# Two columns per product: summing the messages of a graph kernel in two PSUM halves

## Chip, cores and metric

The kernel runs on one core of one Trainium2 chip. The metric is the device time of one launch in microseconds (us), as the median of several runs of the same program; less is better.

## What is computed

The input is a graph of N = 6250 nodes with F = 256 numbers each, and E = 100000 edges, sorted by their destination. Three attention layers follow one another. Cut to what matters:

```python
def gatv2(x, src, dst, Wl, Wr, att, b):     # 4 heads of 64; src, dst with self loops added
    xl, xr = (x @ Wl).reshape(n, 4, 64), (x @ Wr).reshape(n, 4, 64)
    e = leaky_relu(xl[src] + xr[dst], 0.2)
    logits = einsum('ehc,hc->eh', e, att)
    alpha = softmax of logits over the edges of each dst
    return segment_sum(xl[src] * alpha[:, :, None], dst).reshape(n, 256) + b

def gat(h, W, a, src, dst):                 # 8 heads of 32, no self loops
    Wh = h @ W;  s1, s2 = Wh . a[:, :32], Wh . a[:, 32:]
    e = leaky_relu(s1[src] + s2[dst], 0.2)
    attn = softmax of e over the edges of each dst
    return segment_sum(attn[:, :, None] * Wh[src], dst).reshape(n, 256)

h = gatv2(elu(gatv2(x, first weights)), second weights)
x = layernorm(x + h)
return layernorm(x + gat(x, W, a))
```

All numbers are fp32. The part that the change touches is the weighted `segment_sum` at the end of each layer.

## The kernel before

`tile_gnn_kernel` (L634) first makes a plan on the chip (`make_plan`, L699): nodes are sorted by the number of their edges and laid into NB = 49 blocks of 128, one node on each partition. Block b has `cols[b]` edge columns, as many as its busiest node has edges: 38 in the first, then 25, 24, down to 9 in the last, 814 in all. The plan also makes the first layer's table of xl in DRAM. As the graph fits this plan, `tile_by_degree` (L1121) does the rest; another path, for graphs that don't fit, is in the program but not run. Both parts stand under a manual schedule: each engine executes its instructions in the order in which the program text issues them, and an instruction that has to wait holds up all that stand behind it on its engine.

**Layers 1 and 2** are one function, `layer2` (L1261), called for i = 0 and 1; layer 3 is written out from L1445 on in the same form. Each goes once over the 49 blocks. For a block:

- `gather` (L1277, L1451): GpSimd (POOL) issues one indirect DMA per column; each fetches, for all 128 partitions, the table row of that column's source node (256 numbers and some more) into SBUF. The columns of a block are cut into 2 to 5 chunks of at most T = 9 (`chunks`, L1189), each in a row tile g; there are 7 such tiles in layers 1 and 2, and 8 in layer 3. The gathers of block b + 1 are issued ahead of the work on block b. In layers 1 and 2 the node's own row is an additional column, which is not gathered: 814 + 49 = 863 columns a layer.
- `attend` (L1295, L1462): VectorE (DVE) makes the logits lg. In layers 1 and 2 that takes three passes over each chunk (maximum L1302, multiplication L1303, sum L1304). `weights` (L1194) takes the maximum over the columns ("top", L1198), and ScalarE (ACT) the exponentials wt into PSUM: in layers 1 and 2 four instructions, one per head, which sum the denominator den too (L1205); in layer 3 one instruction (L1215), and DVE sums den (L1218).
- `end(b - 1, ...)` (L1317, L1476) finishes the block before: DVE multiplies that block's sum acc, read from PSUM, with its reciprocal den and writes h (L1319, L1478); then follow bias or residual, and in layers 2 and 3 the layer norm's statistics (L1247, L1249), with the root by ACT (L1251).
- DVE takes the reciprocal of den (L1348, L1514).
- `weighted_sum` (L1223): the gathered rows are multiplied in place with their weights. In layers 1 and 2 ACT scales the last 3 to 8 columns, one instruction of 64 numbers for each head and column (L1234), with a copy "by" of the weights; DVE scales the others, a chunk at a time (L1235). Behind the first chunk, `between` runs what is left of block b - 1 on DVE and ACT. Then TensorE (PE) adds the columns: one product of each column with the identity, all accumulating into the same 256 numbers per partition of the PSUM tile acc (L1242). In fp32 a product is two passes, each with a weight load of its own, so that the 863 + 863 + 814 = 2540 products appear as 5080 matmul records. acc has one buffer in layers 1 and 2, and three in layer 3.
- In layers 1 and 2 the last step of block b - 1 comes behind the products of block b: transposes on TensorE, a copy of their result by ACT (xT, L1182), products with the next weights (L1187), a copy of the row by ACT, and its store to DRAM, issued by SyncE (SP). In layer 3 the finished rows y (by ACT, L1259) are written to the output by an indirect DMA from POOL (`put_out`, L1493; L1496), which stands in POOL's order behind the gathers of block b + 1 and writes the rows of block b - 2.

So in each block's order the sum of block b - 1 is taken up by DVE after the logits of block b and ahead of its scalings.

Of the kernel before, what the change touches and what calls it, by code (L numbers as in the profile page):

```python
# [23 lines left out]
F32 = mybir.dt.float32  # L24
# [8 lines left out]
P = 128  # L33
# [1087 lines left out]
def tile_by_degree(  # L1121
# [3 lines left out]
    nc = tc.nc  # L1125
    N, F = x.shape
    H2, D2 = att1.shape
    H1, _, D1 = w3.shape
    NB = -(-N // P)
# [12 lines left out]
    def per_head(t, H):  # L1142
        return t.rearrange("p (h d) -> p h d", h=H)
# [78 lines left out]

    def weighted_sum(ps, rows, cut, wts, H, width, between):  # L1223

        wt, by = wts
        acc = ps.tile([P, F], F32, name="acc")
        S = cut[-1][1]
        for g, (s0, s1) in zip(rows, cut):
            n = s1 - s0
            g4 = g[:, :n, : H * width].rearrange("p t (h d) -> p t h d", h=H)[:, :, :, : F // H]  # L1230
            m = n - by.shape[1] if by is not None and s1 == S else n
            for t in range(m, n):
                for h in range(H):
                    nc.scalar.mul(g4[:, t, h, :], g4[:, t, h, :], by[:, t - m, h : h + 1])  # L1234
            nc.vector.tensor_mul(  # L1235
                g4[:, :m], g4[:, :m],
                wt[:, s0 : s0 + m, :].unsqueeze(3).to_broadcast([P, m, H, F // H]),
            )
            if s0 == 0:
                between()  # L1240
            for t in range(n):
                nc.tensor.matmul(acc, ident, g4[:, t], start=s0 + t == 0, stop=s0 + t == S - 1)  # L1242
        return acc

    def spread_of(work, t):
        stats = work.tile([P, nc.vector.BN_STATS_DIM], F32, name="stats")
# [14 lines left out]
    def layer2(i, table, of, width, start, own, finish):  # L1261

        with ExitStack() as es:
            rowp = es.enter_context(tc.tile_pool(name=f"rows{i}", bufs=7))
            zp = es.enter_context(tc.tile_pool(name=f"z{i}", bufs=3))
            work = es.enter_context(tc.tile_pool(name=f"work{i}", bufs=3))
            ps = es.enter_context(tc.tile_pool(name=f"ps{i}", bufs=2, space=PSUM))  # L1270
            ps1 = es.enter_context(tc.tile_pool(name=f"ps1{i}", bufs=1, space=PSUM))
            pst = es.enter_context(tc.tile_pool(name=f"pst{i}", bufs=2, space=PSUM))
            at = ps1.tile([P, W2], F32, name="at")
            nc.scalar.copy(at, att[i])
            state = {}

            def gather(b):  # L1277
                cut = chunks(cols[b] + 1)
                rows = [rowp.tile([P, T, width], F32, name="g") for _ in cut]
                for g, (s0, s1) in zip(rows, cut):  # L1280
                    for s in range(max(s0, 1), s1):
                        nc.gpsimd.indirect_dma_start(  # L1282
                            out=g[:, s - s0, :], out_offset=None, in_=table,
                            in_offset=source(of, b, s - 1),
                        )
                state[b] = [rows, cut]

            later = []

            def ready(b):  # L1290
                pr, put = own(work, ps, pst, b, state[b][0][0][:, 0, :W2])
                state[b].append(pr)
                later.append(put)

            def attend(b):  # L1295
                rows, cut, xr = state.pop(b)
                S = cols[b] + 1
                lg = work.tile([P, CM + 1, H2], F32, name="lg")
                for g, (s0, s1) in zip(rows, cut):
                    n = s1 - s0  # L1300
                    z = zp.tile([P, T, W2], F32, name="z")[:, :n, :]
                    nc.vector.tensor_max(z, g[:, :n, :W2], xr[:, None, :].to_broadcast([P, n, W2]))  # L1302
                    nc.vector.tensor_mul(z, z, at[:, None, :].to_broadcast([P, n, W2]))  # L1303
                    nc.vector.reduce_sum(  # L1304
                        lg[:, s0:s1, :], z.rearrange("p t (h d) -> p t h d", h=H2), axis=AX.X
                    )
                few = min(S // 3, cut[-1][1] - cut[-1][0] - 1) if b + 1 < NB else 0
                wt, new = weights(work, ps, lg, S, H2, few)
                while later:
                    later.pop()()  # L1310
                if i == 0:
                    for g, (s0, s1) in zip(rows, cut):
                        s = max(s0, 1)
                        nc.scalar.copy(spots[:, b, s - 1 : s1 - 1], g[:, s - s0 : s1 - s0, W2])
                return rows, cut, wt, new

            def end(b, acc, den):  # L1317
                h = work.tile([P, F], F32, name="h")
                nc.vector.tensor_mul(  # L1319
                    per_head(h, H2), per_head(acc, H2),  # L1320
                    den.unsqueeze(2).to_broadcast([P, H2, D2]),
                )
                if i == 0:
                    nc.vector.tensor_add(h, h, bias[0])
                return finish(work, pst, b, h)

            for b in range(3):
                start(work, b)
            gather(0)
            ready(0)  # L1330
            later.pop()()
            if i == 0:
                none(state[0][2])
            acc, den, rest = None, None, None
            for b in range(NB):
                if b + 3 < NB:
                    start(work, b + 3)
                if b + 1 < NB:
                    gather(b + 1)
                if b + 1 < NB:  # L1340
                    ready(b + 1)
                rows, cut, wt, new = attend(b)
                if b:
                    rest = end(b - 1, acc, den)
                if i == 0:
                    nc.vector.tensor_add(x1[:, b, :], x1[:, b, :], bias[1])
                den = new()
                nc.vector.reciprocal(den, den)  # L1348

                last = []  # L1350

                def between():
                    if b:
                        last.append(rest())

                acc = weighted_sum(ps1, rows, cut, wt, H2, D2 + 1, between)
                if i == 0 and b + 1 < NB:
                    none(state[b + 1][2])
                if last:
                    last[0]()  # L1360
            end(NB - 1, acc, den)()()

    def none(t):

# [80 lines left out]
    with ExitStack() as es:  # L1445
        rowp = es.enter_context(tc.tile_pool(name="rows3", bufs=8))
        work = es.enter_context(tc.tile_pool(name="work3", bufs=3))
# [11 lines left out]
                    )  # L1459
            state[b] = (rows, cut)  # L1460

        def attend(b):  # L1462
            rows, cut = state.pop(b)
            S = cols[b]
            lg = work.tile([P, CM, H1], F32, name="lg")
            for g, (s0, s1) in zip(rows, cut):
                nc.vector.tensor_add(
                    lg[:, s0:s1, :], g[:, : s1 - s0, F:],
                    s2[:, b : b + 1, :].to_broadcast([P, s1 - s0, H1]),
                )  # L1470
            nc.vector.scalar_tensor_tensor(
                lg[:, :S, :], lg[:, :S, :], SLOPE, lg[:, :S, :], op0=OP.mult, op1=OP.max
            )
            return rows, cut, *weights(work, ps, lg, S, H1)

        def end(b, acc, den):  # L1476
            h = work.tile([P, F], F32, name="h")
            nc.vector.tensor_mul(  # L1478
                per_head(h, H1), per_head(acc, H1), den.unsqueeze(2).to_broadcast([P, H1, D1])
            )  # L1480
            nc.vector.tensor_add(h, h, x1[:, b, :])
            mv, sd = spread_of(work, h)

            def rest():
                y = work.tile([P, F], F32, name="y")
                layer_norm(y, h, mv, sd)
                return b, y

            return rest
# [14 lines left out]
        acc, den, puts, rest = None, None, {}, None  # L1504
        for b in range(NB):
            if b + 1 < NB:
                gather(b + 1)
            if b - 2 in puts:
                put_out(*puts.pop(b - 2), apart=b + 1 == NB)
            rows, cut, wt, new = attend(b)  # L1510
            if b:
                rest = end(b - 1, acc, den)
            den = new()
            nc.vector.reciprocal(den, den)  # L1514

            def between():
                if b:
                    puts[b - 1] = rest()

            acc = weighted_sum(ps, rows, cut, wt, H1, D1, between)  # L1520
        puts[NB - 1] = end(NB - 1, acc, den)()
        for b in sorted(puts):
            put_out(*puts[b], apart=True)

# [27 lines left out]
```

## Time and profile before

| | |
|---|---|
| three runs | 4039.41, 4051.0, 4052.13 us; median 4051.0 |
| the profiled execution | 4007.86 us, of which 4005.8 are the span of the profile |
| TensorE's granted clock, mean | 0.714 of full speed |
| PE, matmuls | 1932.8 us busy (48%), 6773 records |
| PEld, weight loads | 1480.7 us (37%), 6773 |
| DVE | 2483.7 us (62%), 2510 instructions |
| ACT | 1093.6 us (27%), 4179 |
| POOL | 2490.8 us (62%), 2640 |
| DMA | 399.83 MB, 100 GB/s on average |
| products into acc, L1242 | 5080 records, 1491.8 us busy, 458 ns each on average |
| gathers, L1282 and L1456 | 3 x 814, 947 to 949 ns each on POOL |
| ACT's scalings, L1234 | 2064, 550.0 us busy, 337 ns each |

The profile is of one execution; its times are its own, and the runs differ from it. "Busy" is the time in which an engine's instructions ran, without waits. The matmuls are pipelined and the ends of their records are worked out, not observed. For idle time the profile names what ended it: "issue" where it sees nothing that the engine waited for, "remote" where the release came from something that it could not find, and otherwise the instruction that released it. In a timeline each row is an instruction or a group of like ones: start in us, length in us, engine, line, operation, output<-inputs, shape, how many, and in brackets the idle time ahead of it and what ended it.

### The profile page before, as it was taken

How to read it: one execution, taken by the hardware profiler on the slowest of the kernel's cores; microseconds unless marked ns; L12 is line 12 of the kernel's file. 1: busy time of each engine (PE TensorE's matmuls, PEld its weight loads, DVE VectorE, ACT ScalarE, POOL GpSimd, SP SyncE). 2: the span in 40 equal slices, each digit the busy share in tenths (PEclk: the TensorE clock that was granted, in tenths of full speed). 3: DMA queues.
4: the chain of work that ended last, by engine and by line, in shares of the span. 5: the costliest groups of instructions: out<-in, count | busy, mean ns of one | idle time of the engine just before them, and what ended most of it. 6: DMA issues, size and time to landing. Idle time of an engine off the chain costs nothing.

```text
span 4005.8 us, 26860 instructions
## 1 busy us (share of the span) xinstructions
PE 1932.8 (48%) x6773; PEld 1480.7 (37%) x6773; DVE 2483.7 (62%) x2510; ACT 1093.6 (27%) x4179; POOL 2490.8 (62%) x2640
## 2 busy tenths in 40 slices
PE   5245655566666733454535455543243333333334
PEld 4234444344444522343324344432232232323323
DVE  6278878688888866988859889862232232223233
ACT  2124434344444522333324434430000000000000
POOL 6466666666666536666666666636666665666654
PEclk8667777778878876676667767666666666666667
DMA  7543333333333334333333444324333333333332
GB/s 185 106 94 102 104 100 104 102 101 107 104 105 105 99 76 95 110 107 109 109 107 106 112 111 112 106 65 97 96 96 93 98 86 85 86 87 88 88 84 65
DMA packets 197575, 399.83 MB, mean 100 GB/s; under 512 B 63516, under 2 KB 115994, under 8 KB 197396
## 3 DMA queue, kind: packets, MB, share of 16 engines
q0 software_dynamic: 123488, 342.06, 32.5%
q1 hardware_dynamic: 66226, 54.22, 4.7%
q10 hardware_dynamic: 7698, 1.74, 0.4%
q8 instruction: 58, 0.95, 0.1%
q14 instruction: 105, 0.86, 0.1%
HBM read 357.84 MB, written 40.42 MB: 99 GB/s over the span
## 4 chain that ended last, share of the span: by engine, by line
another core or an unknown queue 24%; PE 23%; issue 20%; DVE 13%; ACT 9%; POOL 8%; DMA 3%; DVEq 0%; ACTq 0%; POOLq 0%; SPq 0%
PE acc L1242 19%; ACT g L1234 4%; DVE z L1303 4%; DVE z L1302 4%; POOL g L1282 4%; PE pm L1187 3%; POOL g L1456 2%; DVE lg L1304 2%; ACT wt L1205 2%; DVE g L1235 1%; POOL near L982 1%; DMA near<-list_d,begin_i 1%; DMA g<-xl_d,spots 1%; ACT xT L1182 1%
## 5 line engine op out<-in xcount | busy, mean ns | idle before, releaser
L1242 PE MATMUL acc<-g,ident 128*128 128x256 f32 x5080 | 1491.8, 458 | 1717.7 <-issue 1215.1
L1242 PEld LDWEIGHTS acc<-g,ident 128*128 128x128 f32 x5080 | 1155.5, 233 | 2053.0 <-issue 1501.3
L1282 POOL DMA_INDIRECT g<-xl_d,spots x814 | 770.6, 947 | 456.3 <-issue 222.7
L1282 POOL DMA_INDIRECT g<-xl_d,near_r x814 | 772.2, 949 | 424.3 <-issue 254.2
L1456 POOL DMA_INDIRECT g<-whs_d,spots x814 | 771.9, 948 | 350.6 <-issue 280.1
L1234 ACT ACTIVATE g<-g,by 128x64 f32<-128x64 f32 x2064 | 550.0, 337 | 329.0 <-issue 327.5
L1235 DVE TENSOR_TENSOR g<-g,wt 128x1792 f32<-128x1792 f32 (+4 forms) x349 | 583.5, 1690 | 2.8
L1478 DVE TENSOR_TENSOR h<-acc,den 128x256 f32<-128x256 f32 x49 | 20.8, 425 | 845.2 <-remote 694.2
L1302 DVE TENSOR_TENSOR z<-g,pr 128x1820 f32<-128x1820 f32 (+4 forms) x236 | 502.4, 2129 | 58.9 <-DMA g<-xl_d,spots 30.9
L1303 DVE TENSOR_TENSOR z<-z,at 128x1820 f32<-128x1820 f32 (+4 forms) x236 | 503.8, 2135 | 8.1
L1304 DVE TENSOR_REDUCE lg<-z 128x28 f32<-128x1820 f32 (+4 forms) x236 | 503.6, 2134 | 8.2
L1251 ACT ACTIVATE sd<-mv,eps 128x1 f32<-128x1 f32 x98 | 28.9, 295 | 931.2 <-DVE mv L1249 801.4
L1182 ACT COPY xT<-pt 128x256 f32<-128x256 f32 x147 | 54.9, 374 | 650.0 <-remote 342.9
L1205 ACT ACTIVATE wt<-lg,top 128x19 f32<-128x19 f32 (+14 forms) x392 | 116.0, 296 | 246.0 <-DVE top L1198 113.1
L1187 PE MATMUL pm<-wh_cat,xT 128*128 128x272 f32 x196 | 80.9, 551 | 181.4 <-issue 122.8
L1496 POOL DMA_INDIRECT out<-y,node_i x49 | 49.6, 1012 | 190.4 <-ACT y L1259 179.6
L1348 DVE RECIPROCAL den<-den 128x4 f32<-128x4 f32 x98 | 17.4, 178 | 235.5 <-ACT wt L1205 165.7
L1187 PE MATMUL pm<-wcat,xT 128*128 128x260 f32 x392 | 132.7, 495 | 55.1 <-ACT xT L1182 53.3
L1319 DVE TENSOR_TENSOR h<-acc,den 128x256 f32<-128x256 f32 x98 | 40.8, 416 | 148.7 <-remote 106.7
L1187 PEld LDWEIGHTS pm<-wcat,xT 128*128 128x128 f32 x392 | 93.4, 251 | 89.0 <-ACT xT L1182 68.6
L1187 PEld LDWEIGHTS pm<-wh_cat,xT 128*128 128x128 f32 x196 | 44.2, 250 | 201.1 <-issue 127.0
L1215 ACT ACTIVATE wt<-lg 128x128 f32<-128x128 f32 (+17 forms) x49 | 14.0, 285 | 251.3 <-DVE lg L1214 198.5
(158 smaller groups left out, 1390.3 us busy)
## 6 DMA issues: line engine op xcount, KB each, us to landing
g<-xl_d,near_r POOLq DMA_INDIRECT x814
g<-xl_d,spots POOLq DMA_INDIRECT x814
g<-whs_d,spots POOLq DMA_INDIRECT x814
whs_d<-row SPq DMA_DIRECT2D x49, 132.0 KB
xl_d<-xl SPq DMA_DIRECT2D x49, 130.0 KB
xl_d<-row SPq DMA_DIRECT2D x49, 130.0 KB
xr_d<-row SPq DMA_DIRECT2D x49, 130.0 KB
two<-xl_d SPq DMA_DIRECT2D x49, 130.0 KB
```

What stands on the lines that cost most here:

```text
L1182: nc.scalar.copy(xT, pt)
L1187: nc.tensor.matmul(pm, xT[:, c, :], w[:, c, :], start=c == 0, stop=c == 1)
L1205: nc.scalar.activation(wt[:, :, h], lg[:, :S, h], AF.Exp, bias=top[:, h : h + 1], accum_out=den[:, h : h + 1],)
L1234: nc.scalar.mul(g4[:, t, h, :], g4[:, t, h, :], by[:, t - m, h : h + 1])
L1235: nc.vector.tensor_mul(g4[:, :m], g4[:, :m], wt[:, s0 : s0 + m, :].unsqueeze(3).to_broadcast([P, m, H, F // H]),)
L1242: nc.tensor.matmul(acc, ident, g4[:, t], start=s0 + t == 0, stop=s0 + t == S - 1)
L1282: nc.gpsimd.indirect_dma_start(out=g[:, s - s0, :], out_offset=None, in_=table, in_offset=source(of, b, s - 1),)
L1302: nc.vector.tensor_max(z, g[:, :n, :W2], xr[:, None, :].to_broadcast([P, n, W2]))
L1303: nc.vector.tensor_mul(z, z, at[:, None, :].to_broadcast([P, n, W2]))
L1304: nc.vector.reduce_sum(lg[:, s0:s1, :], z.rearrange("p t (h d) -> p t h d", h=H2), axis=AX.X)
L1456: nc.gpsimd.indirect_dma_start(out=g[:, s - s0, :], out_offset=None, in_=wh_d[:, :], in_offset=source(spots, b, s),)
L1496: put = nc.gpsimd.indirect_dma_start(out=out[:, :], out_offset=node(b), in_=y, in_offset=None, bounds_check=N - 1, oob_is_err=False,)
```

## The change

acc grows from 256 to 2 x 256 numbers per partition[...]. TensorE takes the columns of a chunk in pairs: one product with 512 numbers a row adds the columns at even places of their chunk to the first half of acc, and those at odd places to the second. The last column of a chunk with an odd number of them is a product of 256 numbers into the first half. So a chunk of 9 has five products in place of nine, and the three layers have 463 + 463 + 437.

The two halves are added when the block is finished: a new `second_half` copies the second one to SBUF by ACT ("half"), because of where it is called ahead of the exponentials of the next block, and behind ACT's earlier work; in `end` DVE adds it to the first half, read from PSUM, into h, and multiplies h with den in place, from SBUF, where before it multiplied acc from PSUM. For the last block the copy is made just ahead of `end`.

```diff
--- before.py
+++ after.py
@@ -1222,8 +1222,9 @@
 
     def weighted_sum(ps, rows, cut, wts, H, width, between):
 
+
         wt, by = wts
-        acc = ps.tile([P, F], F32, name="acc")
+        acc = ps.tile([P, 2, F], F32, name="acc")
         S = cut[-1][1]
         for g, (s0, s1) in zip(rows, cut):
             n = s1 - s0
@@ -1238,9 +1239,18 @@
             )
             if s0 == 0:
                 between()
-            for t in range(n):
-                nc.tensor.matmul(acc, ident, g4[:, t], start=s0 + t == 0, stop=s0 + t == S - 1)
+            for t in range(0, n, 2):
+                k = min(2, n - t)
+                nc.tensor.matmul(
+                    acc[:, :k].rearrange("p k (h d) -> p k h d", h=H), ident, g4[:, t : t + k],
+                    start=s0 + t == 0, stop=s0 + t + k == S,
+                )
         return acc
+
+    def second_half(work, acc):
+        half = work.tile([P, F], F32, name="half")
+        nc.scalar.copy(half, acc[:, 1])
+        return half
 
     def spread_of(work, t):
         stats = work.tile([P, nc.vector.BN_STATS_DIM], F32, name="stats")
@@ -1292,7 +1302,7 @@
                 state[b].append(pr)
                 later.append(put)
 
-            def attend(b):
+            def attend(b, acc):
                 rows, cut, xr = state.pop(b)
                 S = cols[b] + 1
                 lg = work.tile([P, CM + 1, H2], F32, name="lg")
@@ -1304,6 +1314,7 @@
                     nc.vector.reduce_sum(
                         lg[:, s0:s1, :], z.rearrange("p t (h d) -> p t h d", h=H2), axis=AX.X
                     )
+                half = second_half(work, acc) if b else None
                 few = min(S // 3, cut[-1][1] - cut[-1][0] - 1) if b + 1 < NB else 0
                 wt, new = weights(work, ps, lg, S, H2, few)
                 while later:
@@ -1312,12 +1323,13 @@
                     for g, (s0, s1) in zip(rows, cut):
                         s = max(s0, 1)
                         nc.scalar.copy(spots[:, b, s - 1 : s1 - 1], g[:, s - s0 : s1 - s0, W2])
-                return rows, cut, wt, new
-
-            def end(b, acc, den):
+                return rows, cut, wt, new, half
+
+            def end(b, acc, half, den):
                 h = work.tile([P, F], F32, name="h")
+                nc.vector.tensor_add(h, half, acc[:, 0])
                 nc.vector.tensor_mul(
-                    per_head(h, H2), per_head(acc, H2),
+                    per_head(h, H2), per_head(h, H2),
                     den.unsqueeze(2).to_broadcast([P, H2, D2]),
                 )
                 if i == 0:
@@ -1339,9 +1351,9 @@
                     gather(b + 1)
                 if b + 1 < NB:
                     ready(b + 1)
-                rows, cut, wt, new = attend(b)
+                rows, cut, wt, new, half = attend(b, acc)
                 if b:
-                    rest = end(b - 1, acc, den)
+                    rest = end(b - 1, acc, half, den)
                 if i == 0:
                     nc.vector.tensor_add(x1[:, b, :], x1[:, b, :], bias[1])
                 den = new()
@@ -1358,7 +1370,7 @@
                     none(state[b + 1][2])
                 if last:
                     last[0]()
-            end(NB - 1, acc, den)()()
+            end(NB - 1, acc, second_half(work, acc), den)()()
 
     def none(t):
 
@@ -1459,7 +1471,7 @@
                     )
             state[b] = (rows, cut)
 
-        def attend(b):
+        def attend(b, acc):
             rows, cut = state.pop(b)
             S = cols[b]
             lg = work.tile([P, CM, H1], F32, name="lg")
@@ -1471,12 +1483,14 @@
             nc.vector.scalar_tensor_tensor(
                 lg[:, :S, :], lg[:, :S, :], SLOPE, lg[:, :S, :], op0=OP.mult, op1=OP.max
             )
-            return rows, cut, *weights(work, ps, lg, S, H1)
-
-        def end(b, acc, den):
+            half = second_half(work, acc) if b else None
+            return rows, cut, *weights(work, ps, lg, S, H1), half
+
+        def end(b, acc, half, den):
             h = work.tile([P, F], F32, name="h")
+            nc.vector.tensor_add(h, half, acc[:, 0])
             nc.vector.tensor_mul(
-                per_head(h, H1), per_head(acc, H1), den.unsqueeze(2).to_broadcast([P, H1, D1])
+                per_head(h, H1), per_head(h, H1), den.unsqueeze(2).to_broadcast([P, H1, D1])
             )
             nc.vector.tensor_add(h, h, x1[:, b, :])
             mv, sd = spread_of(work, h)
@@ -1507,9 +1521,9 @@
                 gather(b + 1)
             if b - 2 in puts:
                 put_out(*puts.pop(b - 2), apart=b + 1 == NB)
-            rows, cut, wt, new = attend(b)
+            rows, cut, wt, new, half = attend(b, acc)
             if b:
-                rest = end(b - 1, acc, den)
+                rest = end(b - 1, acc, half, den)
             den = new()
             nc.vector.reciprocal(den, den)
 
@@ -1518,7 +1532,7 @@
                     puts[b - 1] = rest()
 
             acc = weighted_sum(ps, rows, cut, wt, H1, D1, between)
-        puts[NB - 1] = end(NB - 1, acc, den)()
+        puts[NB - 1] = end(NB - 1, acc, second_half(work, acc), den)()
         for b in sorted(puts):
             put_out(*puts[b], apart=True)
 
```

## Prediction

> **What bounds the kernel now.** I read the page first, then the busy time of each engine by stage, the waits, and two stretches of the timeline. By stage (start and plan, layer 1, layer 2, layer 3):
>
> ```profile
> span 4005.8 us, 26860 instructions
> 0.00:221.00 221.00, 87.60 (x439) 69.18 (x439) 102.79 (x127) 44.22 (x152) 131.31 (x153) 0.70 0.65 143
> 221.00:1450.00 1229.00, 771.43 (x2670) 570.63 (x2671) 984.82 (x844) 518.64 (x1958) 767.03 (x808) 0.79 0.37 99
> 1450.00:2690.00 1240.00, 601.34 (x2037) 460.85 (x2036) 1015.78 (x824) 462.94 (x1873) 774.81 (x819) 0.69 0.39 105
> 2690.00:4005.80 1315.80, 472.44 (x1628) 380.08 (x1628) 380.29 (x716) 67.78 (x196) 817.68 (x862) 0.66 0.33 89
> ```
>
> The columns are length, then PE, PEld, DVE, ACT, POOL. No engine is full: DVE has 80 and 82% of layers 1 and 2, and POOL, which needs 1.25 us per gather (0.95 and a gap of 0.30), must have 814 x 1.25 = 1018 us a layer. What they wait for:
>
> ```profile
> DVE h L1478 <- remote: 694.2, 25, 37.9
> POOL out L1496 <- ACT y L1259: 179.6, 19, 11.3
> DVE den L1348 <- ACT wt L1205: 165.7, 60, 9.6
> DVE h L1319 <- remote: 106.7, 12, 24.1
> ```
>
> "Remote" is a wait whose releaser the profile could not find. Layer 3 shows what it is:
>
> ```profile
> 3350.34 9.74 PE L1242 MATMUL acc<-g,ident 128*128 128x256 f32 x34 [4.56 <-issue]
> ...
> 3378.97 0.95 POOL L1456 DMA_INDIRECT g<-whs_d,spots  x1 [0.30 <-issue]
> 3385.59 0.42 DVE L1478 TENSOR_TENSOR h<-acc,den 128x256 f32<-128x256 f32 x1 [31.40 <-remote]
> ...
> 3389.84 0.60 ACT L1259 ACTIVATE y<-h,sd 128x256 f32<-128x256 f32 x1 [2.12 <-DVE sd L1256]
> 3390.71 1.01 POOL L1496 DMA_INDIRECT out<-y,node_i  x1 [10.80 <-ACT y L1259]
> ```
>
> The 17 columns are through the array at 3360.08, yet DVE, which needs nothing else, starts 25.5 us later. The trace's semaphore records say why: each column's second pass raises TensorE's semaphore, and these counts arrive late, at 3358.07, 3362.25, 3371.35, 3376.26, 3381.85, 3383.96, 3385.36, all whole multiples of 0.70 us apart, and then five more only 0.042 us apart. The backlog goes when the gathers have stopped; and they stop only because POOL waits for y, which waits for the counts. So every second block of layer 3 costs POOL some 10 us. Layer 1 has the same, and ScalarE is in it:
>
> ```profile
> 1000.65 3.20 ACT L1234 ACTIVATE g<-g,by 128x64 f32<-128x64 f32 x13
> 1004.77 0.35 ACT L1234 ACTIVATE g<-g,by 128x64 f32<-128x64 f32 x1 [0.35 <-issue]
> 1006.17 0.35 ACT L1234 ACTIVATE g<-g,by 128x64 f32<-128x64 f32 x1 [1.05 <-issue]
> 1006.87 0.35 ACT L1234 ACTIVATE g<-g,by 128x64 f32<-128x64 f32 x1 [0.35 <-issue]
> ```
>
> The scalings run at 0.24 us each, then at multiples of 0.70. I read this as TensorE and ScalarE sharing a way out that passes one message per 0.70 us while gathers run long enough. How much it passes per column is the question.
>
> **What the Trainium skill says.** "TensorE: Matmul & The Clock Gate", The cost: per-tile semaphore tail: counts raised by every matmul serialize, at about 26 ns each; one count for several saves the rest. The trace agrees in kind (0.042 us in the bursts), but the slow spells are far beyond that price. "Perfetto Trace Analysis", Tensor Engine Instruction: the end of a matmul's row is computed, and the semaphore follows only once PSUM has acknowledged; it fits that the row's end is 25.5 us before the release. "PSUM — Partial Sum Buffer", The four PSUM rules: a product's output stays within one bank of 512 fp32 numbers, and the first product of a group clears the marks of the whole bank; so a first pair with start opens both halves. No trace here has a 512-wide one into acc.
>
> **The change part by part.** *Products.* Columns 863, 863, 814 become 463, 463, 437 calls (pairs within chunks, odd ones single): 5080 matmul and weight records become 2726 each. Streaming does not shrink: starts in the dense runs lie 216 ns apart for 256 numbers, so a 512-wide pass should take some 430, and 2354 wide passes save perhaps 2.5 ns each: 6 us, not counted. What shrinks is counts and instructions, to 54%.
>
> *ScalarE copy*, 147 times 0.37 us (the xT copy from PSUM, 374 ns). *VectorE add*, 147 times 0.42 (L1478 reads the same shape from PSUM in 425 ns) plus 0.03 gap; the multiplication that follows keeps its price (428 ns from SBUF in L1481).
>
> In layers 1 and 2 the copy stands on ScalarE ahead of the four exponentials; behind it also wait "by" and DVE's L1348. Earlier in ScalarE's order stands the xT copy of the last block, which already waits for TensorE past the same sum, so no new wait arises. The add lies between "top" and L1348, where DVE waits 151.3 us in 48 blocks of layer 1 and 82.6 in 49 of layer 2, and 0.36 us even in the fullest blocks. Per block that leaves 0.1 us (add hidden, 0.45 - 0.36) up to 0.82 (both exposed); taken 0.25, x 98 = 25 us. If the cover goes, 0.45 x 98 = 44.
>
> *Pair at the tail.* Where the last chunk is even (20 blocks a layer), the last product waits for both columns' scalings and runs one column more: 0.43 us at full clock, 0.85 at half. 40 x 0.43 = 17 to 34; part is hidden: 13 us taken.
>
> *Layer 3.* DVE's h now follows a copy and an add: 0.37 + 0.03 + 0.42 + 0.03 = 0.85 us from sum to y. The exponentials wait behind the copy, but are needed only after h, stats and so on. On the path where POOL waits for y, about 27 of 49 blocks: 23 us (0 to 42). Moved past POOL or SP: nothing.
>
> Sum of costs: 25 + 13 + 23 = 61 us (bounds 10 and 156).
>
> *Gain.* Waits tied to late counts: in layers 1 and 2 DVE's idle before L1319 and L1348, 71.3 + 151.3 + 77.4 + 82.6 = 383, less 0.36 x 98 = 35 that stays: 348. In layer 3 POOL's idle before L1496 and L1456 beyond 0.30 each, 190.4 + 302.0 - 0.30 x 859 = 235, less some 10 of ramp: 225. How much goes? In the block shown seven counts are recorded in the 27.3 us from 3358.07 on, about 3.5 us each if one went unrecorded. Some 12 columns pending need 42 us, more than one block of gathers; 6 pairs need 21, and would be through about when POOL runs out at 3379.9. But without the pause the next block starts inside the slow spell, where 9 pairs need 31 us against 22 us of gathers. So I take half of 225: 110. In layers 1 and 2 ScalarE's messages and the other products stay, so 30% of 348: 105. Bounds: 0 (nothing depends on the number) and some 470, where POOL's pace of 1.25 us takes over (1229 - 1079, 1240 - 1093, 1316 - 1142, with 60 to 75 us of ramp in the last two). What is late next is DVE in layers 1 and 2, POOL in layer 3.
>
> Net: 61 - 215 = -154 us. The profiled execution took 4007.9 (span 4005.8), less than the lowest run shown (4039.4); 4007.9 becomes 3854, and the median of 4051 becomes 3897. Predicted 3897.
>
> **Rivals.** *The number of counts does not matter* (slower): the slow spell lasts until gathers pause, whether nine or seventeen counts wait. For it: in layer 3 every long lag ends about 4 us after the last gather. Against it: counts do pass during the spell, and bursts shrink with the block's columns. No gain, costs 61: 4112. It decides wherever less than 61 us come back. *The spell vanishes*: half the messages never fill the way out; 470 - 61 gives 3642, say 3680 as part stays. For it: blocks after a pause pass all counts promptly for 15 us. Against: DVE fills the late blocks of layer 2. *Gain and cost cancel*: about 4051, if only layer 1 and 2 spells ease by some 60 us and POOL, still 3 us a block behind, refills them. That 512 numbers run as two products with a count each is part of the first rival.
>
> **How the numbers follow.** Forecast 0.48 (own range 3800 to 4000), vanishing 0.10, cancelling 0.10, number irrelevant 0.32. Within 0.3% (12 us, what a measurement of this kernel can tell from no change) lies the cancelling case: 0.10. Faster 0.48 + 0.10 and 0.02 of the irrelevant case with all costs hidden and something won: 0.60; slower 0.30. The range 3700 to 4125 leaves out part of the vanishing case and costs well above 61.
>
> **What would show it.** Right: 2726 matmul records in acc, wide passes near 430 ns; DVE's "remote" wait before h in layer 3 well below 694 us, POOL's before out below 180; the scalings less often at 0.70. Wrong: the waits before h end as before, just after the gathers pause, with h 0.8 us later; or passes slower than 430 ns; or ScalarE standing at the copy with exponentials queued.

## The result and the profile after

The changed kernel takes 4152.27 us (median of 4 runs, 4138.48 to 4193.21) against 4046.57 us before (4 runs, 4039.41 to 4052.13): a ratio of 1.0278, 95% interval 1.0215 to 1.0341. It is slower by 2.8%, where 3897 us had been predicted, and it lies outside the predicted range.

The page's first line and the table by stage (start, layers 1, 2, 3; columns as before the change: length, PE, PEld, DVE, ACT, POOL, clock, DMA share, GB/s):

```profile
span 4147.3 us, 23041 instructions
0.00:221.00 221.00, 88.26 (x438) 69.64 (x439) 101.42 (x125) 42.13 (x143) 129.50 (x150) 0.69 0.67 142
221.00:1531.00 1310.00, 755.51 (x1876) 391.46 (x1876) 1006.52 (x890) 526.58 (x2020) 772.00 (x811) 0.77 0.35 93
1531.00:2845.00 1314.00, 629.37 (x1230) 279.74 (x1230) 1032.17 (x877) 490.70 (x1921) 773.25 (x814) 0.68 0.37 98
2845.00:4147.30 1302.30, 465.49 (x874) 202.85 (x874) 401.25 (x765) 81.34 (x245) 825.84 (x866) 0.67 0.34 90
```

Layer 1 takes 1310 us instead of 1229, layer 2 1314 instead of 1240, layer 3 1302 instead of 1316. The weight loads fell (PEld 570.6 to 391.5 us in layer 1), the matmuls' busy time did not (771.4 to 755.5), and nobody is fuller: DVE has 77 and 79% of layers 1 and 2 where it had 80 and 82. So the lost time is waiting. The waits:

```profile
ACT half L1252 <- remote: 740.4, 25, 68.0
DVE h L1491 <- ACT half L1252: 467.1, 25, 42.1
ACT g L1235 <- issue: 382.3, 443, 1.8
DVE h L1491 <- issue: 320.8, 24, 41.8
DVE h L1330 <- ACT half L1252: 301.7, 22, 36.2
POOL g L1292 <- PE acc L1244: 219.9, 44, 15.7
POOL out L1510 <- ACT y L1269: 166.5, 15, 18.2
```

L1491 and L1330 are the new adds (layer 3; layers 1 and 2), L1252 is the copy. The late counts of TensorE are still there: they now hold up the copy, and the add behind it, as they held up the multiplication before. POOL's wait for y has hardly fallen (179.6 to 166.5 us). ScalarE's scalings are slowed more, not less (327.5 to 382.3 us). And POOL's waits for a row tile that the profile puts to TensorE, 105.7 us before and at most 11.4 long, are now 219.9 us and up to 15.7 long. One late block of layer 2 shows how it looks, with the other engines' rows left out:

```profile
2446.18 7.68 PE L1244 MATMUL acc<-g,ident 128*128 128x512 f32 x12 [8.69 <-issue]
...
2446.70 3.44 ACT L1235 ACTIVATE g<-g,by 128x64 f32<-128x64 f32 x14
...
2450.90 0.35 ACT L1235 ACTIVATE g<-g,by 128x64 f32<-128x64 f32 x1 [0.77 <-issue]
2452.33 0.35 ACT L1235 ACTIVATE g<-g,by 128x64 f32<-128x64 f32 x1 [1.08 <-issue]
...
2461.18 0.95 POOL L1292 DMA_INDIRECT g<-xl_d,spots  x1 [0.30 <-issue]
...
2463.07 2.07 PE L1244 MATMUL acc<-g,ident 128*128 128x512 f32 x2 [5.99 <-remote]
...
2465.42 0.95 POOL L1292 DMA_INDIRECT g<-xl_d,spots  x1 [3.29 <-PE acc L1244]
2465.61 0.37 ACT L1182 COPY xT<-pt 128x256 f32<-128x256 f32 x1 [9.10 <-PE pt L1180]
```

POOL gathers without a pause worth the name through the block's products and scalings (the longest idle time is 1.48 us). The scalings fall back to one in 1.4 us, the last pair starts at 2463.07, 6.6 us after the last scaling has ended, and only when POOL has run out of row tiles does the rest come through.

### The profile page after: what moved, and what is told of

It is laid out like the page before. It is cut to its first block, busy times and chain, and to the rows that moved or that the text cites. A ratio compares the mean times of both kernels' runs of the same rounds, so it can differ in the third digit from the quotient of the medians.

```text
span 4147.3 us, 23041 instructions
## 1 busy us (share of the span) xinstructions
PE 1938.6 (47%) x4418; PEld 943.7 (23%) x4419; DVE 2541.4 (61%) x2657; ACT 1140.8 (28%) x4326; POOL 2500.6 (60%) x2640
## 4 chain that ended last, share of the span: by engine, by line
issue 28%; another core or an unknown queue 19%; PE 17%; DVE 14%; POOL 12%; ACT 7%; DMA 3%; DVEq 0%; POOLq 0%; ACTq 0%; SPq 0%
PE acc L1244 14%; POOL g L1292 6%; POOL g L1468 4%; DVE z L1312 3%; DVE z L1313 3%; ACT g L1235 3%; PE pm L1187 3%; DVE g L1236 2%; DVE lg L1314 2%; POOL near L982 1%; DMA near<-list_d,begin_i 1%; ACT wt L1205 1%; DMA g<-xl_d,near_r 1%; PE pt L1180 1%
## 5 line engine op out<-in xcount | busy, mean ns | idle before, releaser
L1244 PE MATMUL acc<-g,ident 128*128 128x512 f32 (+1 forms) x2726 | 1500.0, 709 | 1883.5 <-issue 1275.2
L1244 PEld LDWEIGHTS acc<-g,ident 128*128 128x128 f32 x2726 | 621.3, 238 | 2738.3 <-issue 2172.9
L1235 ACT ACTIVATE g<-g,by 128x64 f32<-128x64 f32 x2064 | 552.4, 337 | 384.6 <-issue 382.3
L1491 DVE TENSOR_TENSOR h<-half,acc 128x256 f32<-128x256 f32 x49 | 20.6, 421 | 787.9 <-ACT half L1252 467.1
L1330 DVE TENSOR_TENSOR h<-half,acc 128x256 f32<-128x256 f32 x98 | 40.7, 415 | 482.0 <-ACT half L1252 301.7
L1252 ACT COPY half<-acc 128x256 f32<-128x256 f32 x147 | 56.1, 382 | 982.1 <-remote 740.4
L1510 POOL DMA_INDIRECT out<-y,node_i x49 | 49.6, 1013 | 176.9 <-ACT y L1269 166.5
L1187 PE MATMUL pl<-wcat,xT 128*128 128x260 f32 x196 | 64.7, 458 | 54.0 <-ACT xT L1182 45.3
L982 POOL DMA_INDIRECT near<-list_d,begin_i x49 | 60.5, 1234 | 32.9 <-DVE begin_i L977 18.3
L1479 DVE TENSOR_TENSOR lg<-g,s_r 128x56 f32<-128x56 f32 (+4 forms) x113 | 19.9, 214 | 97.4 <-DMA g<-whs_d,spots 83.9
```

The costliest lines, as they stand in the source:

```text
L982: nc.gpsimd.indirect_dma_start(out=near[:, k, :], out_offset=None, in_=listed, in_offset=bass.IndirectOffsetOnAxis(ap=begin_i[:, k : k + 1 ...
L1187: nc.tensor.matmul(pm, xT[:, c, :], w[:, c, :], start=c == 0, stop=c == 1)
L1244: nc.tensor.matmul(acc[:, :k].rearrange("p k (h d) -> p k h d", h=H), ident, g4[:, t : t + k], start=s0 + t == 0, stop=s0 + t + k == S,)
L1252: nc.scalar.copy(half, acc[:, 1])
```

## The experiments

For each kernel I give the median and its ratio to the kernel before, measured on the same chip, and from its profile the length of each layer's gathers: from the start of the layer's first gather to the start of its last. 814 gathers at 1.25 us make 1018 us; the rest is POOL waiting, and its node loads in layer 1 and output writes in layer 3. (In the later batches the kernel before had medians of 4041.57 to 4043.78; each ratio is to its own. Most differences are under 2%, so they are read from their intervals; the layers are those of one profile each.)

| kernel | median us | ratio (95%) | layer 1 | layer 2 | layer 3 |
|---|---|---|---|---|---|
| before | 4046.57 | 1 | 1253 | 1177 | 1283 |
| changed | 4152.27 | 1.0278 (1.0215 to 1.0341) | 1328 | 1254 | 1262 |
| e1_singles | 4071.66 | 1.0098 (1.0059 to 1.0136) | 1261 | 1183 | 1315 |
| e2b_dve | 4154.82 | 1.0286 (1.0262 to 1.0310) | 1306 | 1276 | 1259 |
| e3_tail | 4121.23 | 1.0195 (1.0173 to 1.0217) | 1288 | 1257 | 1264 |
| e4_third | 4014.81 | 0.9936 (0.9913 to 0.9960) | 1261 | 1185 | 1263 |
| e5_first_single | 4025.04 | 0.9956 (0.9934 to 0.9979) | 1261 | 1180 | 1267 |
| e6_rest_single | 4079.38 | 1.0082 (1.0056 to 1.0107) | 1277 | 1221 | 1257 |
| e7_pause12 | 4030.50 | 0.9968 (0.9949 to 0.9987) | 1264 | 1196 | 1261 |
| e8_pause3 | 3975.58 | 0.9820 (0.9787 to 0.9852) | 1271 | 1185 | 1239 |
| e9_one | 4033.02 | 0.9971 (0.9957 to 0.9985) | 1270 | 1191 | 1278 |
| e10_two | 4011.18 | 0.9915 (0.9879 to 0.9950) | 1261 | 1188 | 1264 |
| e11_pair_one | 4010.72 | 0.9903 (0.9875 to 0.9931) | 1261 | 1187 | 1254 |
| e12_pair_two | 3988.01 | 0.9836 (0.9794 to 0.9878) | 1272 | 1184 | 1246 |

The layers repeat well: those whose code is that of before (e4, e8 to e12) take 1261 to 1272 and 1184 to 1191 us in layers 1 and 2, so differences under some 10 us say nothing, and the profiled execution of before, with 1253 and 1177, lies below all of them. With pairs in layers 1 and 2 single layers may move more: the changed kernel and e2b, alike in total, differ by 22 us in each, one up and one down.

### Which part costs

Three theories stood first: A, that h now waits behind ScalarE's queue; B, that the last pair of a block waits for two columns that ScalarE scales; C, the prediction's own, by which fewer counts are a gain and copy and add the cost. A count, here and below, is the raising of TensorE's semaphore by one product.

**e1_singles**: copy and add stay, the pairs go.

```diff
-            for t in range(0, n, 2):
...
+            for t in range(n):
                 nc.tensor.matmul(
...
+                    acc[:, t % 2], ident, g4[:, t], start=s0 + t == 0, stop=s0 + t == S - 1,
                 )
```

> The changed kernel with one product of 256 numbers per column again, columns alternating between the two halves; ScalarE's copy and VectorE's add stay. So it has all 2540 products and counts of the kernel before, and all that the change costs beside them. Theory A (the loss is that h now stands behind ScalarE's copy, and so behind all that ScalarE has queued): no better than the changed kernel, about 4150 us, since fewer counts gain nothing. Theory B (the loss is the pair at the tail: the last product waits until ScalarE has scaled two columns): most of the loss gone, about 4070. Theory C (as the prediction had it, halving the counts is a gain and copy and add cost 61): worse than the changed kernel, 4250 or more.

Measured 4071.66. Copy and add alone cost 8 and 6 us in layers 1 and 2, no more than what repeats, and 32 us in layer 3 (1283 to 1315). So the pairs themselves cost 67 and 71 us in layers 1 and 2 (1261 to 1328, 1183 to 1254), and gain 53 in layer 3 (1315 to 1262). Theory A fails, and C too, except in layer 3. The total is the one that theory B named, 4070; whether for B's reason, e3 tests.

**e2b_dve**: no copy by ScalarE; `second_half` is dropped and the add becomes

```diff
-nc.vector.tensor_add(h, half, acc[:, 0])
+nc.vector.reduce_sum(h, acc.rearrange("p k f -> p f k"), axis=AX.X)
```

> The changed kernel without ScalarE's copy: VectorE sums the two halves with one reduction straight from PSUM into h, so h waits for TensorE alone, as before the change. Theory A: the loss of layers 1 and 2 goes, about 4030 us, with VectorE's wait before h named TensorE or remote again. Theory B: hardly changed, 4120 to 4150. Theory C: about 40 less than the changed kernel, 4110.

Measured 4154.82, as the changed kernel (just above B's range; C's outcome is missed by 45). That h stands behind ScalarE's queue, conspicuous as it is in the waits, is not the cause.

**e3_tail**: pairs only among the columns that VectorE scales (m of the chunk's n).

```diff
-            for t in range(0, n, 2):
-                k = min(2, n - t)
+            t = 0
+            while t < n:
+                k = 2 if t + 2 <= m else 1
...
+                t += k
```

> The changed kernel with pairs only among the columns that VectorE scales; the 3 to 8 columns of a block that ScalarE scales in layers 1 and 2 are single products into the first half again, so the last product waits for one column as before. Layer 3 as in the changed kernel. Theory A: as the changed kernel, 4130 to 4160. Theory B: about 4060. Theory C: 13 us less than the changed kernel at most, or more time through more counts.

Measured 4121.23: 31 us less than the changed kernel, where theory B expected some 90. In these profiles layer 1 gets 40 us back (1328 to 1288) and layer 2 nothing (1254, 1257), but layers with pairs also move by 22 us without such a reason. The pairs of ScalarE's columns are a part of the loss; more than half of it lies elsewhere. (The edit gives those columns their single counts back too, so it doesn't show that the waiting for two of them is what costs.)

**e4_third**: pairs, copy and add in layer 3 only; `layer2` is that of before.

```diff
-            for t in range(0, n, 2):
-                k = min(2, n - t)
+            for t in range(0, n, 2 if H > 4 else 1):
+                k = min(2 if H > 4 else 1, n - t)
```

> Pairs, copy and add in layer 3 only; layers 1 and 2 as before the change. All theories: layers 1 and 2 take what they took before. From the two profiles, layer 3's gathers take 1262 us with the change against 1283, so about 4025 us; if that difference is chance, 4045 to 4070.

Measured 4014.81, ratio 0.9936: in layer 3 the change is a small gain, as the two profiles said.

### Why the pairs cost in layers 1 and 2

POOL waits in nearly every block of layers 1 and 2 until a row tile is free again. Before the change the profile puts these waits mostly to three releasers:

```profile
POOL g L1282 <- ACT g L1234: 113.5, 28, 9.4
POOL g L1282 <- PE acc L1242: 105.7, 49, 11.4
POOL g L1282 <- remote: 98.7, 31, 5.7
```

The order of the gathers and the 7 tiles tell which tile it is: of the idle times over 1.8 us before a gather (without the start of layer 2), 39 of 45 in layer 1 and 31 of 48 in layer 2 stand before the tile of some block's first chunk. The start of layer 2 shows what pairs do to such a wait. It begins with a block of 39 columns in 5 chunks; POOL fills all 7 row tiles and then needs the first one back, that is, TensorE's counts of the first chunk's 7 columns. First the kernel before, then the changed one:

```profile
1524.43 10.94 PE L1242 MATMUL acc<-g,ident 128*128 128x256 f32 x40 [68.00 <-issue]
1524.73 0.95 POOL L1282 DMA_INDIRECT g<-xl_d,spots  x1 [0.30 <-issue]
1534.43 0.94 POOL L1282 DMA_INDIRECT g<-xl_d,spots  x1 [8.76 <-PE acc L1242]
```

```profile
1606.53 6.83 PE L1244 MATMUL acc<-g,ident 128*128 128x512 f32 x11 [67.22 <-DMA g<-xl_d,spots]
1606.90 0.95 POOL L1292 DMA_INDIRECT g<-xl_d,spots  x1 [0.30 <-issue]
1612.34 0.95 POOL L1292 DMA_INDIRECT g<-xl_d,spots  x1 [4.49 <-PE acc L1244]
```

With seven counts the tile is free 10.0 us after the first product, with four after 5.8. POOL's pause shrinks from 8.8 to 4.5 us. Pauses are when late counts get through: in layer 1 before the change, 533 of the 924 counts that the trace recorded during the gathers fall into the 185 us of such pauses, and 429 of the 432 that follow the one before within 0.1 us. Before the change layer 2 settles, for the most part, in a rhythm: a block's gathers (22 down to 10), a pause of 2 to 4 us, the next block's gathers. With pairs the rhythm breaks: runs of 5 to 51 gathers, and 14 pauses of more than 6 us beyond the usual distance of gathers where there were 3 (12 and 4 in layer 1). The pauses do not become fewer: those over 1.8 us are 48 and 45 in layers 1 and 2, against 45 and 48, but they sum to 255 and 238 us instead of 185 and 173. A regular short pause has given way to irregular ones, some of them long. I took this as theory F and tested it.

**e5_first_single** and **e6_rest_single**: in layers 1 and 2 only the first chunk of each block is taken column by column, or all but the first.

```diff
-            for t in range(0, n, 2):
-                k = min(2, n - t)
+            step = 1 if H <= 4 and s0 == 0 else 2      # e6: s0 > 0
+            for t in range(0, n, step):
+                k = min(step, n - t)
+                j = t % 2
...
```

> The changed kernel, in which layers 1 and 2 take the columns of each block's first chunk one by one (256 numbers, alternating between the halves) and the others in pairs; layer 3 in pairs. Theory F (before the change GpSimd pauses once in each block, because the counts of the first chunk, whose row tile it waits for, come late; that pause lets the backlog through; pairs bring these counts early, GpSimd runs on, and the slow spells build up): the first chunk alone restores the pauses, layers 1 and 2 near 1261 and 1183 us of gathers as with single products throughout, total about 4050. Theory G (pairs cost where TensorE waits for ScalarE's columns, at the end of the block): as the changed kernel, 4130 to 4160.

> The reverse: in layers 1 and 2 the first chunk in pairs and all other chunks one by one. Theory F: the first chunk's counts come early, the loss stays, 4110 to 4150. Theory G: most of the loss goes, about 4050.

e5 measured 4025.04, layers 1 and 2 at 1261 and 1180 us: with the first chunk's counts given back, the whole loss is gone, although all the other chunks, the end of the block included, still go in pairs. Theory G fails. Nor is it the number of products that decides: e5 has 624 in each of these layers, e6 702, and e5 is the faster. e6 measured 4079.38, with 1277 and 1221: more than half of the loss goes there too, which F did not expect (4110 to 4150). In the first block of layer 2 the two differ as F says (e5, then e6):

```profile
1533.39 12.93 PE L1246 MATMUL acc<-g,ident 128*128 128x256 f32 x31 [67.62 <-issue]
...
1543.27 0.95 POOL L1294 DMA_INDIRECT g<-xl_d,spots  x1 [8.70 <-PE acc L1246]
```

```profile
1555.50 7.80 PE L1246 MATMUL acc<-g,ident 128*128 128x512 f32 x18 [67.71 <-DMA g<-xl_d,spots]
...
1561.41 0.95 POOL L1294 DMA_INDIRECT g<-xl_d,spots  x1 [4.65 <-PE acc L1246]
```

9.9 us against 5.9. In e6's layer 2 the steady rhythm is nevertheless found again for some 14 blocks in a row, and lost later. Long pauses are as rare there as before the change (3 over 6 us), yet the layer takes 38 us more than in e1: the long pauses are not the whole of the loss.

**e7_pause12**: the changed kernel, with a pause made on purpose behind each block's gathers in layers 1 and 2.

```diff
+                for _ in range(3):
+                    nc.gpsimd.memset(rest_i, 0.0)      # 128x1024 numbers
```

> The changed kernel with three GpSimd memsets of 128x1024 numbers behind the gathers of each block in layers 1 and 2, some 3 us in which no gather is issued (nothing else is changed; the memsets are work added). Theory F: the pauses are given back on purpose and the long ones go: layers 1 and 2 at 1018 + 147 us plus some ramp, about 1260 and 1190, total about 4050. Theory G: the pause is added to the loss or hides in it, 4150 to 4300.

Measured 4030.50, layers at 1264 and 1196 us: added work of 2 x 49 x 2.9 us takes 2.9% off the changed kernel's time. Three pauses of more than 6 us are left in layer 2 of 14, and one in layer 1 of 12. POOL's stops over 1.8 us sum to 199 and 192 us with the memsets counted in, close to the 185 and 173 of before. That is the plainest sign that what was lost was the regular pause.

### Layer 3: what a pause is worth, and what the number of counts is worth

Here, from block 17 on, POOL before the change meets no row tile for which it has to wait long, and runs into the wait for y instead.

**e8_pause3, e9_one, e10_two**: the kernel before with three, one or two memsets behind each block's gathers in layer 3. **e11_pair_one, e12_pair_two**: the same with e4_third for a base.

```diff
+            for _ in range(3):                         # e9, e11: 1; e10, e12: 2
+                nc.gpsimd.memset(rest_i, 0.0)
             state[b] = (rows, cut)
```

> The kernel before, with the same three memsets behind the gathers of each block in layer 3 alone. There GpSimd stops 11 us in every second block, until the late counts are through. Theory F: a pause of 3 us in each block keeps the counts prompt, the 205 us of stalls shrink to the 147 of the pauses and some 20, total 4000 to 4030. If only a wait for TensorE itself helps, not the pause: 205 + 147 us, about 4190.

> The kernel before with one memset of 128x1024 (0.96 us) behind the gathers of each block of layer 3. GpSimd's own work there is 1018 us of gathers, 61 of output writes, 49 of memsets. Theory F, if a pause of 1 us lets a block's 17 counts through: about 1150 us of layer 3 and 3900 in all. If the backlog needs more, slow spells and the wait for y come back in part: 3960 to 4040.

> The same with two memsets in each block (1.9 us). Theory F: 1018 + 61 + 94 and some 20, layer 3 about 1195 us, total about 3935, unless the counts need longer; then it is no better than the three memsets' 3976.

> Pairs, copy and add in layer 3 alone, layers 1 and 2 as before the change, and one memset (0.96 us) behind the gathers of each block of layer 3. If the number of counts sets how long a pause must be, half the counts need half of it: 3900 to 3920 here, clearly less than with one memset and single products. If the number doesn't matter: as that kernel or up to 30 us more, for copy and add.

> The same with two memsets. If the number of counts matters: spells are gone and GpSimd's work alone sets layer 3, about 3935 us. If not: as with single products and two memsets, or up to 30 us more.

With three, 3975.58 us, the fastest of all kernels here: 1.8% under the kernel before (ratio 0.9787 to 0.9852), and under the 4000 to 4030 that F expected. POOL's groups show it, first the output writes before the change, then memsets and writes in e8; the number behind the second bar is the idle time ahead of the group:

```profile
L1496 POOL DMA_INDIRECT out<-y,node_i x49 | 49.6, 1012 | 190.4 <-ACT y L1259 179.6 <-issue 10.8
```

```profile
L1464 POOL MEMSET rest_i<- 128x1024 f32 x147 | 140.9, 958 | 5.6
L1500 POOL DMA_INDIRECT out<-y,node_i x49 | 50.6, 1032 | 24.2 <-ACT y L1259 16.5 <-issue 4.6 <-DVE top L1198 1.2
```

190.4 us of idle time before the writes have become 24.2, for 140.9 of memsets; now POOL's own work bounds the layer. The counts are still late: VectorE's idle time before h in layer 3 is 493 us against 845 before, but POOL no longer stands for it. One or two memsets were not enough, against my first expectation of 3900 and 3935: 4033.02 and 4011.18. With pairs they were not enough either: 4010.72 and 3988.01, where 3900 to 3920 and 3935 were expected if the number of counts mattered. That is 22 and 23 us less than with single products, copy and add paid for, so the number has a small effect; one memset with pairs is no clear gain over none (e4, 4014.81). The waits for y before the output writes, with single products and one or two memsets, then pairs and one or two:

```profile
L1500 POOL DMA_INDIRECT out<-y,node_i x49 | 50.1, 1023 | 153.2 <-ACT y L1259 147.3 <-issue 5.9
```

```profile
L1500 POOL DMA_INDIRECT out<-y,node_i x49 | 49.9, 1018 | 96.8 <-ACT y L1259 90.6 <-issue 6.0 <-DVE lg L1472 0.2
```

```profile
L1512 POOL DMA_INDIRECT out<-y,node_i x49 | 49.9, 1018 | 142.5 <-ACT y L1269 132.7 <-issue 6.0 <-DVE g L1236 3.8
```

```profile
L1512 POOL DMA_INDIRECT out<-y,node_i x49 | 49.8, 1017 | 78.2 <-ACT y L1269 71.5 <-issue 6.7
```

The rhythm of the long stops, 9 to 17 us beyond the usual distance of gathers (the output write of 1.3 us and the memsets included), says it better. Of the later blocks every second has one with single products and no memset, every second with one memset (every third towards the end), every third with two, and with three there is a single one in the layer. With pairs every third without a memset (the changed kernel), every third with one, about every fifth with two. I read this as a backlog that is carried over from block to block: a block adds its counts to it, each pause takes some off, and when it stands too high POOL has to stop until it is gone. Half the counts let POOL run half as long again. The number of counts does matter, but a long stop still comes, and is longer when it comes (11 to 16 us in the changed kernel's late blocks, 8.5 to 12.4 before).

## Why the prediction was wrong, step by step

- **Products**: right. 2726 records, and wide passes start 0.43 us apart.
- **Copy and add in layers 1 and 2**: taken 25 us, measured 14 (e1), which is within what repeats. **In layer 3**: taken 23, measured 32, within the bounds.
- **Pair at the tail**: taken 13 us; e3 got 31 back, a part of the 138 below, by undoing all pairs of ScalarE's columns and not the last alone. I had priced the last product's longer pass. In a slow spell it also waits for eight scalings instead of four; that this is the 31 is not shown. (19 blocks a layer have an even last chunk, not 20.)
- **Gain in layer 3**: taken 110 us, measured 53. Fewer counts did help, but half as much as taken. I had seen that without the pause the next block starts inside the slow spell, but not that the backlog adds up over blocks, so that every third block stops instead of every second, and for longer.
- **Gain in layers 1 and 2**: this step fails. The prediction put it as "ScalarE's messages and the other products stay, so 30% of 348: 105". Measured is a loss of 138 (67 + 71, changed against e1). The sum has the late counts as a cost only, and puts at nothing what an earlier count does to POOL, which waits for the row tiles that TensorE releases. In these layers the late counts of the first chunk also did something useful: they made POOL pause for a short time in nearly every block. With the first chunk in pairs that rhythm is lost, and POOL's pauses grow from 185 to 255 and from 173 to 238 us. Single products in the first chunk alone (e5), or a pause put in by memsets (e7), bring the layers back to 1261 and 1180, or 1264 and 1196 us. The waits of POOL for its row tiles were in the profile of before, 318 us in three lines; it was idle time of an engine that seemed to have time to spare, and I didn't ask what it was good for.
- **The sum with measured terms**: 14 + 32 - 53 + 138 = 131 us. As all terms are differences along before, e1 and changed, this must be the difference of the layers in the two profiles (75 + 77 - 21), and is no test of them. The medians differ by 106, as the profiled execution of before was a low one.
- **Rivals**: "the number of counts does not matter" gave the right side, at 4112 us, but by luck: its costs alone give 4072 (e1), and the loss has another cause. Its argument was that in layer 3 every long lag ends about 4 us after the last gather. Of VectorE's waits of more than 10 us before h there, 22 of 26 ended 3 to 7 us after POOL's last gather; of ScalarE's before the copy in the changed kernel only 14 of 31 ended so late. So with half the counts more blocks get through while gathers run.
- **Its signs**: the wait before h in layer 3 hardly fell (788 us in all, 467.1 + 320.8, against 845, of which 694 were "remote"), POOL's before out fell by 13 us only, the scalings were slowed more.
- **The price of a count**: the Trainium skill, "TensorE: Matmul & The Clock Gate", The cost: per-tile semaphore tail, has about 26 ns for each count of a packed group of products. The bursts here are of that order (0.042 us). Under gathers it is not the price: the counts of layer 3 then come mostly at multiples of 0.70 us, and of the intervals above 1.3 us a quarter are longer than 4.90 us before and 6.30 us after the change (some of them hold time in which no product was due). The measurement decides: in this kernel the price of a count depends on whether POOL is issuing gathers.

What stays open: why messages wait while POOL issues gathers (no trace here shows the resource); why e6 wins back more than half; how the tail and the pauses share the loss; and whose late message ended POOL's pauses in layer 1, where the profile names ScalarE's scalings for 28 of the 45 before the change. It is not shown either that a regular pause works by keeping the slow spells short: scalings of ScalarE that start 0.5 to 3 us after the one before are 271 and 171 in layers 1 and 2 with the change, 88 and 98 in e7, but 390 and 157 in e5, which has lost no time. A single count at the end of each chunk was not tried, nor pairs with three memsets in layer 3.

## What to carry to other kernels

A short, regular wait of an engine can be worth keeping: here TensorE's late counts got through in it. Before shortening a product or releasing a buffer sooner, look at who pauses on that release, and what passes in the pause. Where a queue must pause anyway, a small pause placed on purpose in each block can be cheaper than the long one that comes by itself: in layer 3, 2.9 us a block took the place of about 10 us in every second.

## What the runs showed of the hardware that I had not expected

TensorE's counts come in bursts as soon as POOL stops issuing gathers: more than half of those recorded in layer 1 fall into 15% of its time (533 of 924 in 185 of 1253 us). In layer 3 a pause of about 1 us a block (0.96 us of memset) brought little, and 2.9 us took POOL's wait for y from 179.6 to 16.5 us with 9 to 38 counts a block. With one count for two columns the same stop came after 3 blocks instead of 2.
